# A transformer block on one core: self-attention's output projection in seven half-size products over pairs of units

## The chip, the core and the metric

The kernel runs on one NeuronCore of a Trainium2 chip. A core has five engines that work side by side, each in the order of its own instruction queue: TensorE (PE in the profile; PEld is its loading of weights) multiplies matrices out of on-chip memory (SBUF) into eight accumulation banks (PSUM); VectorE (DVE), ScalarE (ACT) and GpSimd (POOL) work on rows of 128 partitions; SyncE (SP) issues the transfers, which 16 DMA engines carry out. Engines wait for each other through semaphores. The metric is the time of one execution on the device in microseconds (us), the median of three runs. All data are 32-bit floats; a 32-bit product shows as two matmul records in the trace.

## What is computed

The reference, cut to what matters:

```python
h = layernorm(x, ln1);  x = attention(h, h, sa_wq, sa_wk, sa_wv, sa_wo, sa_bo) + x
h = layernorm(x, ln2);  x = attention(h, cond, ca_wq, ca_wk, ca_wv, ca_wo, ca_bo) + x
h = layernorm(x, ln3);  p = h @ ff_w1 + ff_b1
a, gate = p[..., :1024], p[..., 1024:]
out = (a * gelu(gate)) @ ff_w2 + ff_b2 + x

def attention(xq, xkv, wq, wk, wv, wo, bo):     # 16 heads of 64
    q, k, v = xq @ wq, xkv @ wk, xkv @ wv
    return softmax(q k^T / 8, per head) v @ wo + bo
```

x is 2 x 1024 x 256 (two batches of 1024 tokens), the context 2 x 154 x 192, the attention width 1024. The output projection `@ wo` takes 1024 values a token to 256, and its result is added to x.

## The kernel before

**Units and steps.** The self-attention goes by 16 *units*: a batch b and a pair of heads pr (8 pairs a batch). A unit is 8 *steps*, so the stage has 128 (`SA`), numbered p; n is the step within a unit, ui the unit. In step p the main loop first does `self_first`: TensorE multiplies the scores of two groups of 64 query rows, for two heads and 1024 keys, into two PSUM tiles of 128 x 1024 (`scores`, L502); VectorE takes the maxima (L511); ScalarE takes the exponentials with their sums (L517); SyncE sends maxima and sums between partitions in four small transfers, the *exchange* (L527); one step later GpSimd works out differences and denominators (L535 to L546), two steps later VectorE takes reciprocals (L614) and GpSimd multiplies the weights (`weighted`, L622), and VectorE turns them (L649) into the tile that the value products read (L556). At the end of a step TensorE gets one more piece of work: the value products of half a half-unit (64 products, steps 0, 3, 4 and 7 of a unit), or, in steps 1, 2, 5 and 6, what `run_work` takes from the lists `work` (the next unit's queries, keys and values), `side` (normalizations of the other batch or the next stage) and `outs` (output projections). Order on each engine is the program's order.

**The output projection.** The 8 pairs of a batch make four groups `og` of two pairs (`HP` = 2, `NQ` = 4). Outputs of a group are kept transposed in a tile `oT` of 2 x 1024 columns (two buffers in rotation), its weights in a tile `wo` of 2 x 256 columns (two buffers, `load_out`). When a group is done, `self_beside` appends `out_piece`s, two in each of the next two units: a piece takes two token tiles of 128, four products of 256 columns (L476), and one addition to x on VectorE (L483), which the main loop does one step later from `adds`. They run in step 6 of units 2 to 14 and step 2 of unit 15; the last group of batch 1 runs as four pieces early in the cross-attention.

**The cross-attention** goes by the same 16 units in 48 steps c (three a unit): scores on context keys `kT` (L876), softmax without an exchange, turned weights, value products (L941), queries of the next unit, output projections. The context keys of pairs 0 to 5 are made during the first self-attention units, those of pairs 6 and 7 in its last step but one (p = SA - 2). `kT` holds all of them, 8 x 320 columns, in SBUF for both stages. At the end the feed-forward takes its two products in seven half-size products for eight (L1046, L1167), in the manner of Strassen and Winograd; `kT` then serves it as a buffer.

**Biases** are added to x on GpSimd (L323) from the list `later`, one at steps 2, 4 and 6 from unit 4 on. **Transfers** all go through SyncE's queue in the program's order, with eight semaphores in rotation. `load_ahead` places the weights of the unit after next at steps 2, 3 and 7, and the output weights at step 6 of every second unit. Normalized inputs of a stage are in tiles `hT`, one for each batch (two buffers): batch 0's self-attention tile is followed in its buffer by batch 0's cross-attention tile.

Of the kernel before, what the change touches and what calls it, by code (L numbers as in the profile page):

```python
# [13 lines left out]
P = 128  # L14
# [4 lines left out]
def tile_transformer_block(ctx: ExitStack, tc: tile.TileContext, a: dict, out: bass.AP):  # L19
# [165 lines left out]
    kT = const.tile([P, NPAIR, B * TP], F32, tag="kT", name="kT")  # L185

# [34 lines left out]
    def norm_pieces(kind, b, first=False):  # L221
# [11 lines left out]
        def stats(t):  # L233
            if t == 0:
                st["hT"] = hT[kind, b] = p2.tile(
                    [P, nh, NC * S // nh], F32, tag="hT", name=f"hT_{ln}_{b}")
# [39 lines left out]
        def turn(t):  # L276
# [10 lines left out]
            def store():  # L287
                k = NC * 2 * P // nh
                for c in range(nh):
                    own = st["hT"][:, c, t // 2 * k:(t // 2 + 1) * k]  # L290
# [38 lines left out]
    def norm_beside(kind, b):  # L329
# [12 lines left out]
        for k in range(NT // n + 3):  # L342
            tiles = tile_order(kind)[k * n:(k + 1) * n]
            needs = [(after, b, half, t) for half in range(NQ) for t in tiles if after]
# [16 lines left out]
    def two_banks(name):  # L361
        return [mm_tile(f"{name}_{r}") for r in range(2)]
# [79 lines left out]
    def self_queries(b, pr, m=KB, t0=0):  # L442
        pq = two_banks(f"pq_sa{b}_{pr}")
# [227 lines left out]

    def self_values(h, part):

        b, pr = units[h // 2]
        if part == 0:
            halves[h, "po"] = [sum_tile(f"po_{h}_{a2}") for a2 in range(2)]
            if pr % HP == 0 and h % 2 == 0:
                oT["sa", b, pr // HP] = pt_.tile([P, HP, S], F32, tag="oT", name=f"o_sa{b}_{pr}")
# [43 lines left out]
    def self_beside(ui):  # L722
# [16 lines left out]
        if ui == NPAIR + 1:  # L739
            norm_beside("ca", 0)  # L740

    def load_ahead(p):
# [19 lines left out]
        if p == SA - SH - 6:  # L762
            load_keys(6, 2)

# [94 lines left out]
    def cross_pieces(b, pr):  # L859

        return [
            costing(2, lambda: cross_queries(b, pr, KB)),
# [3 lines left out]
    def cross_first(c):  # L866
# [4 lines left out]
        q, k = qk["ca", b, pr], kT[:, pr, b * TP:b * TP + T]  # L871
        sc = ps_s.tile([P, 2, HB], F32, tag="s", name=f"sc_{c}")
# [329 lines left out]
    with tc.manual_schedule():  # L1202
# [61 lines left out]
        for p in range(SA):  # L1264
# [16 lines left out]
            load_ahead(p)  # L1281
            if p < 2 * SH - 1 or p % SH in (1, 2):

                run_work(2 if p < SA - SH else 1, n > SH or p < SH, sum_tile)
# [4 lines left out]
                elif p == SH + 2:  # L1289
                    run(lambda: together(*(  # L1290
                        lambda pr=pr: context_keys(pr, sum_tile) for pr in (3, 4))))
                    flush(stores)
                elif p == SA - 2:
                    run(lambda: context_values(*units[0]))
                    for pr in (6, 7):
# [175 lines left out]
```

## Time and profile before

| | us |
|---|---|
| median of 3 runs | 1072.77 (1072.15 to 1073.38) |
| the profiled execution | 1073.1 |
| its span, first to last instruction | 1071.3 |
| TensorE busy | 1059.9 (99%) |
| VectorE busy | 879.9 (82%) |
| GpSimd busy | 766.8 (72%) |
| ScalarE busy | 653.3 (61%) |
| self-attention's output projection, TensorE busy | 59.8, 256 records of 386 ns |
| feed-forward's second product in half-size products, TensorE busy | 58.5 over five groups, 448 records of 275 ns |

Busy time is the union of an engine's records, each with its modelled end; consecutive records overlap, so durations of single matmuls add up to more than the time they take, and the distance between starts is the better measure of pace. "A <-B" behind an idle time names what ended it. In a list of groups the columns are line, engine, operation, output <- inputs with shapes, count, busy time and mean, and idle time before them; in a timeline, start, duration, engine and line; in the chain of waits, start, duration and what the end of the program was waiting for. A row of the stretches gives the busy time of PE, PEld, DVE, ACT and POOL with counts, then the granted clock, the DMA share and GB/s.

### The profile page before, as it was taken

Reading aid. Unit: us, or ns where it says so; the run is one execution under the profiler, and the core shown is the slowest. Engines: PE = TensorE matmul, PEld = TensorE weight load, DVE = VectorE, ACT = ScalarE, POOL = GpSimd, SP = SyncE. Lnnn points to the kernel's source line nnn. Section 1 sums busy time; section 2 is a strip of 40 time slices with the busy share of each in tenths; the row PEclk is TensorE's granted clock in tenths of the full one; section 3 lists DMA queues with packets and bytes.
Section 4 is the critical chain, followed back from the end, with each engine's and each line's share of the span. In section 5 each row is a group of like instructions: output and inputs, shape, how many; then the busy total and the mean of one; then the engine's idle time right before and its main releaser. Section 6 shows DMA issues by size and latency. Waiting matters only on the chain.

```text
span 1071.3 us, 46097 instructions
## 1 busy us (share of the span) xinstructions
PE 1059.9 (99%) x19108; PEld 707.8 (66%) x19108; DVE 879.9 (82%) x1293; ACT 653.3 (61%) x2089; POOL 766.8 (72%) x1604
## 2 busy tenths in 40 slices
PE   8999999999999999999999999999999999999998
PEld 6545557566566565665665656566777767889998
DVE  5789999998989989989999898978776777765654
ACT  5666767667766666666667766666556655243221
POOL 2677777778777777777776776758766678598783
PEclk9999999999999999999999999999999999999999
DMA  3232122111111111211211211125523221000000
GB/s 95 64 92 64 46 48 46 34 44 24 43 43 35 43 44 25 58 30 35 48 31 34 48 29 38 24 68 132 131 60 83 68 58 41 1 6 16 21 10 31
DMA packets 99235, 50.57 MB, mean 47 GB/s; under 512 B 30218, under 2 KB 97810, under 8 KB 99026
## 3 DMA queue, kind: packets, MB, share of 16 engines
q1 hardware_dynamic: 97698, 46.96, 17.9%
q8 instruction: 151, 2.47, 1.0%
q10 hardware_dynamic: 1328, 0.66, 0.2%
q14 instruction: 58, 0.48, 0.2%
HBM read 35.25 MB, written 3.41 MB: 36 GB/s over the span
## 4 chain that ended last, share of the span: by engine, by line
PE 89%; DVE 4%; ACT 2%; POOL 2%; DMA 1%; issue 1%; SPq 1%; DVEq 0%; POOLq 0%; ACTq 0%
PE s L502 20%; PE po L556 19%; PE py_sa L476 5%; PE py_ca L476 5%; PE pv_sa L402 5%; PE pq_sa L371 5%; PE pk_sa L371 5%; PE pf L1167 4%; PE pq_ca L371 4%; PE poc L941 4%; PE pb L1046 4%; PE sc L876 3%; PE pa L1046 2%; PE pc L1046 2%; DMA st<-st 1%; PE ph_ln L283 1%
## 5 line engine op out<-in xcount | busy, mean ns | idle before, releaser
L622 POOL TENSOR_SCALAR p<-p,rd,ee 128x512 f32<-128x512 f32 x508 | 386.4, 771 | 96.9 <-DVE rd L614 93.7
L517 ACT ACTIVATE p<-s,st 128x512 f32<-128x512 f32 x512 | 345.7, 686 | 178.0 <-DVE st L511 174.7
L511 DVE TENSOR_REDUCE st<-s 128x2 f32<-128x1024 f32 x256 | 308.4, 1206 | 52.5 <-issue 20.4
L649 DVE STREAM_TRANSPOSE pT<-p 128x1024 f32<-128x1024 f32 x256 | 302.2, 1218 | 1.5 <-POOL p L622 1.5
L502 PE MATMUL s<-k_sa,q_sa 64*32 64x512 f32 x4096 | 255.2, 591 | 2.6 <-ACT p L517 1.9
L556 PE MATMUL po<-pT,v_sa 64*32 64x256 f32 x8192 | 238.6, 376 | 0.8 <-ACT p L894 0.8
L556 PEld LDWEIGHTS po<-pT,v_sa 64*32 64x32 f32 x8192 | 175.2, 106 | 72.9 <-issue 26.8
L502 PEld LDWEIGHTS s<-k_sa,q_sa 64*32 64x32 f32 x4096 | 81.4, 106 | 103.1 <-issue 54.0
L894 ACT ACTIVATE p<-sc,neg 128x154 f32<-128x154 f32 x256 | 97.1, 405 | 72.2 <-DVE rden L902 65.8
L905 POOL TENSOR_SCALAR p<-p,rden 128x154 f32<-128x154 f32 x256 | 97.2, 404 | 52.5 <-DVE rden L902 51.6
L517 ACT ACTIVATION_READ_ACCUMULATOR p<-s,st 128x1 f32 x512 | 103.4, 202 | 0.0
L535 POOL TENSOR_TENSOR dd<-st 128x8 f32<-128x8 f32 x128 | 26.0, 203 | 68.9 <-DMA st<-st 65.0
L402 PEld LDWEIGHTS pv_sa<-sa_wv,hT_ln 64*128 64x128 f32 x1024 | 58.5, 188 | 14.2 <-issue 10.1
L881 DVE TENSOR_REDUCE neg<-sc 128x6 f32<-128x924 f32 (+1 forms) x48 | 48.1, 1002 | 20.2 <-PE sc L876 20.0
L402 PE MATMUL pv_sa<-sa_wv,hT_ln 64*128 64x128 f32 x1024 | 61.7, 275 | 0.0
L476 PE MATMUL py_ca<-ca_wo,o_ca 128*128 128x256 f32 x256 | 61.1, 385 | 0.0
L476 PE MATMUL py_sa<-sa_wo,o_sa 128*128 128x256 f32 x256 | 59.8, 386 | 0.0
L476 PEld LDWEIGHTS py_sa<-sa_wo,o_sa 128*128 128x128 f32 x256 | 47.2, 190 | 18.0 <-ACT v_sa L411 5.9
L371 PE MATMUL pq_ca<-hT_ln,ca_wq 64*128 64x512 f32 (+1 forms) x352 | 57.7, 589 | 0.0
L371 PE MATMUL pq_sa<-hT_ln,sa_wq 64*32 64x512 f32 (+1 forms) x976 | 57.2, 586 | 0.0
L371 PE MATMUL pk_sa<-hT_ln,sa_wk 64*32 64x512 f32 x960 | 56.6, 590 | 0.0
L894 ACT ACTIVATION_READ_ACCUMULATOR p<-sc,neg 128x1 f32 x256 | 56.5, 221 | 0.0
(132 smaller groups left out, 1451.0 us busy)
## 6 DMA issues: line engine op xcount, KB each, us to landing
v_sa<-v_sa SPq DMA_DIRECT2D x32, 256.0 KB, 3.8
st<-st SPq DMA_DIRECT2D x510, 1.0 KB, 1.8
v_ca<-vd SPq DMA_DIRECT2D x32, 160.0 KB, 3.4
sa_wq<-in_L_xattn_sa_wq_dram SPq DMA_DIRECT2D x32, 128.0 KB, 3.6
sa_wk<-in_L_xattn_sa_wk_dram SPq DMA_DIRECT2D x32, 128.0 KB, 3.6
sa_wv<-in_L_xattn_sa_wv_dram SPq DMA_DIRECT2D x32, 128.0 KB, 3.3
ca_wq<-in_L_xattn_ca_wq_dram SPq DMA_DIRECT2D x32, 128.0 KB, 3.4
wf<-in_L_xattn_ff_w_dram SPq DMA_DIRECT2D x12, 256.0 KB, 5.9
```

Source lines behind the costliest of these rows:

```text
L371: nc.tensor.matmul(pq[r][f:f + m, at:at + n], lhsT=wt[own, c, f:f + m], rhs=h[own, c, t0:t0 + n], start=(c == 0), stop=(c == NH - 1), tile ...
L402: nc.tensor.matmul(pv[r][:, i * P:(i + 1) * P], lhsT=h[own, c, i * P:(i + 1) * P], rhs=wt[own, c, :], start=(c == 0), stop=(c == NH - 1), ...
L476: nc.tensor.matmul(py[:, e * D:(e + 1) * D], lhsT=o[:, i, (t + e) * P:(t + e + 1) * P], rhs=wo[kind, b, g][:, i, :], start=(i == 0), stop= ...
L502: nc.tensor.matmul(sc[a4 * KB:(a4 + 1) * KB, j, :], lhsT=q[r, c:c + KB], rhs=k[r, h * HB:(h + 1) * HB], start=True, stop=True, tile_positi ...
L511: nc.vector.tensor_reduce(st[:, 0, 0, i, :], sc, AX.X, ALU.max, negate=True)
L517: nc.scalar.activation(pr[:, j, :], sc[:, j, :], AF.Exp, bias=st[:, 0, 0, i, j:j + 1], accum_out=st[:, 0, 1, i, j:j + 1],)
L556: nc.tensor.matmul(po[a2][d:d + KB, :QH // 2], lhsT=v[r, t, e, d:d + KB], rhs=pT[r, d // DH * NK + n, :], start=(t == 0 and e == 0), stop= ...
L622: nc.gpsimd.tensor_scalar(pr[:, j, :], pr[:, j, :], v["rd"][:, c:c + 1], v["ee"][:, 0, c:c + 1], op0=ALU.mult, op1=ALU.mult,)
L649: nc.vector.transpose(halves[h][:, :, c:c + KB], slot[p]["members"][i].rearrange("p j (n k) -> p (j n) k", k=KB))
L894: nc.scalar.activation(pr_[:, j, i, :T], sc[:, j, i * T:(i + 1) * T], AF.Exp, bias=neg[:, j, i:i + 1], accum_out=den[:, j, i:i + 1],)
L905: nc.gpsimd.tensor_scalar(pr_[:, j, i, :T], pr_[:, j, i, :T], rden[:, j, i:i + 1], 1.0, op0=ALU.mult, op1=ALU.mult,)
L1046: nc.tensor.matmul(into[:, :BT], lhsT=lhs, rhs=wh[pair][i], start=first, stop=True, skip_group_check=True)
```

## The change

A batch's four groups make two halves of two groups. Batch 0's two halves and batch 1's first (groups 0 and 1) are now projected in seven half-size products instead of eight; batch 1's second half stays in whole pieces.

A *block* n takes two token tiles (t0 and t0 + 2) and the two groups of a half as a 2 x 2 matrix of blocks A, and the two groups' weights, each split into its left and right 128 columns, as B. `weight_blocks` makes five sums of B on GpSimd once for a half, `token_blocks` five sums of A on GpSimd for each block, `out_block` multiplies seven products of 128 columns (two instructions each) into two PSUM tiles, and returns three functions that add the results to x on VectorE: one addition of 512 columns and four of 256, in three steps one after another.

Block n belongs to unit n + 4, so blocks 0 to 11 run in units 4 to 15; their products are emitted in step 6 (the last one in step 2 of unit 15), their GpSimd sums one to two in a step from step 0 on. Both weight tiles of a half are loaded in step 7 of units 3, 7 and 11. Units 2 and 3 have no output projection. Batch 1's groups 2 and 3 are eight whole pieces from the first step of the cross-attention on.

Since outputs of two groups must be kept for four units more, four homes hold them: groups 0 and 1 in the two `oT` buffers, group 2 in `kT`'s first 2048 columns, and group 3 in the batch's own `hT` buffer (`homes`), which the last unit's projections no longer need. So the context keys are all made by step 22, stored in device memory (`kd`) at step 24, and loaded back whole at cross step 6; the first four units' keys come back into small tiles near the end of the self-attention. The rest of `kT` and a part of `ends` hold weight sums, the tile of context-key weights holds token sums. Queries of the self-attention and the first cross unit use the value banks (`sum_tile`), so that the two `mm` banks can hold a block's results. The second normalization takes the token tiles in another order, and starts in unit 10 in place of 9.

The diff, cut to its core:

```diff
+    kd = dram.tile([P, NPAIR, B * TP], F32, name="kd")
+    homes = [p2.tile([P, NC * S], F32, tag="hT", name=f"home{b}") for b in range(B)]
@@ tile_order
+        if kind == "ca":
+            return [t for r in range(TF) for i in range(r, NT // 2, TF) for t in (i, NT // 2 + i)]
+    def parts_of(kind, b):
+        if kind == "sa":
+            return ("s0", "s1") if b < B - 1 else ("s0", NQ - 2, NQ - 1)
+        return range(NQ)
@@ self_pieces
-            return self_queries(b, pr)
+            return self_queries(b, pr, bank=sum_tile)
+    def hold_outputs(b, og):
+        if og == NQ - 2:
+            flat = kT.rearrange("p a b -> p (a b)")[:, :HP * S]
+        elif og == NQ - 1:
+            flat = homes[b]
+        else:
+            oT["sa", b, og] = pt_.tile([P, HP, S], F32, tag="oT", name=f"o_sa{b}_{og}")
+            return
+        oT["sa", b, og] = flat.rearrange("p (i s) -> p i s", i=HP)
+    NBLK = NT // 2
+    def weight_blocks(n):
...
+        tt = nc.gpsimd.tensor_tensor
+        return [
+            lambda: tt(t1, b11, b22, ALU.add),
+            lambda: tt(t3, b12, b22, ALU.subtract),
+            lambda: tt(b12, b11, b12, ALU.add),
+            lambda: tt(t4, b21, b11, ALU.subtract),
+            lambda: tt(b21, b21, b22, ALU.add),
+        ]
+    def token_blocks(n):
...
+        return [
+            lambda: tt(s1, a11, a22, ALU.add),
+            lambda: tt(s2, a21, a22, ALU.add),
+            lambda: tt(s5, a11, a12, ALU.add),
+            lambda: tt(a21, a21, a11, ALU.subtract),
+            lambda: tt(a12, a12, a22, ALU.subtract),
+        ]
+    def out_block(n):
...
+        for own, at, m in ((px, 1, 3), (px, 2, 4), (px, 3, 6), (px, 0, 7), (py, 0, 1), (py, 1, 5), (py, 2, 2)):
+            for c in range(HP):
+                nc.tensor.matmul(
+                    own[:, at, :], lhsT=sums_t[n][m][:, c, :], rhs=sums_w[m][:, c, :],
+                    start=(c == 0), stop=(c == HP - 1), skip_group_check=True)
...
+        def first():
+            take(square, px.rearrange("p (j d) k -> p j d k", d=2))
+        def second():
+            take(diagonal, px[:, 2:0:-1, :])
+            take(diagonal, py[:, 0:1, :].broadcast_to([P, 2, P]))
+        def third():
+            take(other, py[:, 1:3, :])
+            take(diagonal, py[:, 1:3, :], ALU.subtract)
@@ self_beside
-        if ui >= HP:
-            ob, og = divmod((ui - HP) // HP, NQ)
-            t0 = (ui % HP) * 2
-            out_pieces("sa", ob, og, out_order("sa")[t0:t0 + 2])
@@ load_ahead
-        if n == 2 * SH - 2 and ui % HP == 1 and p < SA - 2:
-            k = ui // HP
-            load_out("sa", *divmod(k, NQ))
+        half = ui // NBLK
+        if n == 2 * SH - 1 and ui % NBLK == NBLK - 1 and ui < NU - 1:
+            for og in range(2 * half % NQ, 2 * half % NQ + 2):
+                load_out("sa", 2 * half // NQ, og)
+        if p == SA - SH - 1:
+            for og in (NQ - 2, NQ - 1):
+                load_out("sa", B - 1, og)
-        if p == SA - SH - 6:
+        if p == 2 * SH + 1:
             load_keys(6, 2)
+        if p == 6 * SH:
+            nc.sync.dma_start(out=kd, in_=kT)
+        if p == SA - 2 * SH:
+            crossed["first"] = one.tile([P, 3, TP], F32, tag="xn", name="k_first")
+            nc.sync.dma_start(out=crossed["first"], in_=kd[:, :3, :TP])
+        if p == SA - SH - 1:
+            nc.sync.dma_start(out=ends[:, HP * P:HP * P + TP], in_=kd[:, 3, :TP])
@@ the main loop, self-attention
+            block, at = ui - NBLK, n
+            if block == NU - NBLK - 1 and n != 2:
+                block = None
+            elif block == NU - NBLK - 2 and n == 2 * SH - 1:
+                block += 1
+            if block is not None and block >= 0:
+                if n == 0 and block % NBLK == 0:
+                    summing.extend(weight_blocks(block))
+                if n == (2 * SH - 1 if block == NU - NBLK - 1 else 0):
+                    summing.extend(token_blocks(block))
+            steps = 2 if ui >= NU - 1 or n == 2 * SH - 1 else -(-len(summing) // max(6 - n, 1))
+            for _ in range(min(steps, len(summing))):
+                summing.pop(0)()
             if p < 2 * SH - 1 or p % SH in (1, 2):
-                run_work(2 if p < SA - SH else 1, n > SH or p < SH, sum_tile)
+                if block is not None and block >= 0 and n == (2 if ui == NU - 1 else 2 * SH - 2):
+                    adds.extend(out_block(block))
+                turns = n > SH or p < SH or n == 2 and NU - NBLK <= ui < NU - 1
+                run_work(2 if p < SA - SH else 1, turns, sum_tile)
+                elif p == 5 * SH + 2:
+                    run(lambda: together(*(
+                        lambda pr=pr: context_keys(pr, sum_tile) for pr in (6, 7))))
                 elif p == SA - 2:
                     run(lambda: context_values(*units[0]))
-                    for pr in (6, 7):
-                        run(lambda: context_keys(pr, sum_tile))
@@ the main loop, cross-attention
+                for og in (NQ - 2, NQ - 1):
+                    out_pieces("sa", B - 1, og, out_order("sa"))
             if c == SH:
-                out_pieces("sa", B - 1, NQ - 1, out_order("sa"))
             if c == 0:
                 run(lambda: self_values(2 * NU - 2, 1))
+                run_work(2, 0)
-                if ui > 1:
+                if ui:
                     run_work(0, 0, n_sum=1)
-            if c == 0:
-                load_out("sa", B - 1, NQ - 1)
+            if c == 2 * len(CG):
+                nc.sync.dma_start(out=kT, in_=kd)
```

More of the change, by code (lines that the diff above doesn't have):

```diff
@@ L289, in store @@
                 for c in range(nh):
-                    own = st["hT"][:, c, t // 2 * k:(t // 2 + 1) * k]
+                    at = t // 2 if kind == "ff" else order[t] % (NT // 2)
+                    own = st["hT"][:, c, at * k:(at + 1) * k]
                     turned = ph[c * n // nh][:, c % (nh // n) * k:][:, :k]
@@ L343, in norm_beside @@
             tiles = tile_order(kind)[k * n:(k + 1) * n]
-            needs = [(after, b, half, t) for half in range(NQ) for t in tiles if after]
+            needs = [(after, b, half, t) for half in parts_of(after, b) for t in tiles if after]
             def step(fns):
@@ L677, in self_values @@
             if pr % HP == 0 and h % 2 == 0:
-                oT["sa", b, pr // HP] = pt_.tile([P, HP, S], F32, tag="oT", name=f"o_sa{b}_{pr}")
+                hold_outputs(b, pr // HP)
         po = halves[h, "po"]
```

53 lines of the change are left out of this document (45 added, 8 removed).

## The prediction

> **What bounds the kernel now.** I read first the share of the span by engine and the chain of work that ended last, on the page: the span is 1071.3 us, the same execution took 1073.1 us (1.8 us lie around the span), and the median of the runs shown is 1072.77, so a sum made on this execution is lowered by 0.3 us at the end. About 0.2%, 2.1 us, is what a measurement of this kernel can tell from no change.
>
> ```profile
> PE 1059.9 (99%) x19108; PEld 707.8 (66%) x19108; DVE 879.9 (82%) x1293; ACT 653.3 (61%) x2089; POOL 766.8 (72%) x1604
> PE 89%; DVE 4%; ACT 2%; POOL 2%; DMA 1%; issue 1%; SPq 1%; DVEq 0%; POOLq 0%; ACTq 0%
> ```
>
> TensorE is the chain almost everywhere, at full clock. Next come the timelines of one self-attention step (unit 8, its first step), engine by engine: a step is two score groups, then either 64 value products or a projection or an output projection.
>
> ```profile
> 350.19 1.95 PE L502 MATMUL s<-k_sa,q_sa 64*32 64x512 f32 x32
> 352.07 3.72 PE L476 MATMUL py_sa<-sa_wo,o_sa 128*128 128x256 f32 x16
> 355.72 1.95 PE L502 MATMUL s<-k_sa,q_sa 64*32 64x512 f32 x32
> 360.91 1.92 PE L502 MATMUL s<-k_sa,q_sa 64*32 64x512 f32 x32
> 366.08 1.92 PE L502 MATMUL s<-k_sa,q_sa 64*32 64x512 f32 x32
> ...
> 362.17 1.21 DVE L511 TENSOR_REDUCE st<-s 128x2 f32<-128x1024 f32 x1
> 363.30 0.15 DVE L614 RECIPROCAL rd<-den 128x4 f32<-128x4 f32 x1
> 366.77 0.65 DVE L483 TENSOR_TENSOR x<-py_sa,x 128x512 f32<-128x512 f32 x1
> 367.34 1.21 DVE L511 TENSOR_REDUCE st<-s 128x2 f32<-128x1024 f32 x1
> ```
>
> A plain step is 366.08 - 360.91 = 5.17 us of TensorE; the one with the output projection is 355.72 - 350.19 = 5.53. VectorE needs, without the addition, 366.77 - 362.17 = 4.60 us, and 5.17 with it (367.34 - 362.17). So TensorE bounds the stage, VectorE is 0.57 us behind it, and a step that TensorE has less for can shrink by that and no further than 4.60.
>
> **The change part by part.**
>
> *The products.* Each of 12 blocks replaces 8 products of 256 columns (two records each) by 14 of 128 columns. That is 16 records against 28, in the same slot of a unit. The second kind is seen in the feed-forward, in the chain's own view:
>
> ```profile
> 1043.30 0.89 PE pf L1167 x8
> 1055.83 11.22 PE pf L1167 x98
> 307.21 0.59 PE ph_ln L283 x4
> ...
> L476 PEld LDWEIGHTS py_sa<-sa_wo,o_sa 128*128 128x128 f32 x256 | 47.2, 190 | 18.0 <-ACT v_sa L411 5.9
> ```
>
> The long run gives 11.22/98 = 0.1145 us a record, 3.21 for 28; a run that follows the narrow score tiles pays an entry (four transposes of the same shape took 0.59 where 0.45 is due), so I take 3.29 against 5.53 - 1.88 = 3.65 now, -0.36 a block, **-4.3 us**. Ends: 3.12 (the eight-record run) gives -6.4, and 3.35 gives -3.6. [...]
>
> *Units 2 and 3.* They held two output projections each and now hold none (blocks run in units 4 to 15). Their step 6 falls from 5.53 to VectorE's 4.60 at best: -0.93 each, and 0 at worst; I take **-1.5 us** together, since VectorE waits a little in most steps. Context keys 6 and 7 go into unit 2's emptied slot and cost nothing there.
>
> *Four more output projections in the cross-attention.* The last half of batch 1 stays in whole products: eight pieces now run after the self-attention, where four did.
>
> ```profile
> 693.52 2.32 PE L786 MATMUL pk<-ctxT,ca_wk 96*128 96x320 f32 x8
> 711.56 0.80 PE L556 MATMUL po<-pT,v_sa 64*32 64x256 f32 x17 [0.85 <-ACT p L894]
> ...
> 716.23 3.61 PE po L556 x128
> ...
> 720.83 3.65 PE py_sa L476 x16
> ...
> 725.21 1.92 PE py_sa L476 x8
> ...
> 722.00:760.00 38.00, 37.91 (x447) 26.35 (x446) 31.37 (x74) 23.92 (x115) 29.09 (x76) 1.00 0.49 124
> ```
>
> TensorE works 37.91 of 38 us there, so nothing hides them. Two pieces at the first cross step cost 3.65, less the 0.85 us gap that they fill, less at most 0.5 for the context keys (2.32 us) that leave the last self step but one, which VectorE then holds at 4.60. Two more come one at a time, at cross steps 5 and 8: 1.85 each. Together **+5.9 us** (ends 4.5, if the chain through ScalarE hides a piece, and 7.4, all four).
>
> So TensorE alone comes out level: -4.3 - 1.5 + 5.9 = +0.1.
>
> *The sums on GpSimd.* Each block adds five additions of 128x256, and the first block of a half five more on its weights: 75 in all.
>
> ```profile
> L323 POOL TENSOR_TENSOR x<-x,sa_bo 128x256 f32<-128x256 f32 x16 | 11.7, 733 | 0.0
> ...
> 400.54 1.52 POOL L622 TENSOR_SCALAR p<-p,rd,ee 128x512 f32<-128x512 f32 x2 [0.81 <-DMA st<-st]
> 404.32 0.20 POOL L546 TENSOR_TENSOR den<-zz 128x4 f32<-128x4 f32 x1
> 405.72 1.52 POOL L622 TENSOR_SCALAR p<-p,rd,ee 128x512 f32<-128x512 f32 x2 [1.20 <-DVE rd L614]
> ```
>
> GpSimd's own step is 404.52 - 400.54 = 3.98 us, so 1.2 of 5.17 are free and one addition of 0.73 fits: nine units place one in each of five steps, hidden, **+0.4 us** where a bias addition falls into the same step (ends 0 and 3). In units 4, 8 and 12 two additions stand in each of four steps, 1.45 us, 0.26 too much each time, and the first waits for both weight matrices, which SyncE now issues one step before, behind the exchange and the value weights.
>
> ```profile
> 364.21 1.36 SPq L134 DMA_DIRECT2D sa_wv<-in_L_xattn_sa_wv_dram  x2
> sa_wo<-in_L_xattn_sa_wo_dram SPq DMA_DIRECT2D x8, 256.0 KB, 3.6
> wf<-in_L_xattn_ff_w_dram SPq DMA_DIRECT2D x12, 256.0 KB, 5.9
> 367.70 0.20 POOL L546 TENSOR_TENSOR den<-zz 128x4 f32<-128x4 f32 x1
> 368.73 1.52 POOL L622 TENSOR_SCALAR p<-p,rd,ee 128x512 f32<-128x512 f32 x2 [0.84 <-DVE rd L614]
> ```
>
> In unit 8's first step SyncE is free at 365.57; two issues of 0.6 and 3.6 to landing put the second matrix at 369.85, where GpSimd, at the end of its step, wants it at 367.90. Queued behind the waiting addition are the weightings of the next step, due at 368.73, then the differences and denominators; VectorE's reciprocal and transposes wait for those, ScalarE for VectorE, TensorE for ScalarE. Two additions end at 371.30: GpSimd is 2.6 late. A matrix that lands 1.2 sooner gives 1.4; I take 1.9. The three further double steps add 0.26 each, in units 4 and 8 also 0.72 for a bias addition and 0.26 for the next: 3.7, 3.7 and 2.7 late. What of that TensorE feels:
>
> ```profile
> 404.33 1.20 DVE L511 TENSOR_REDUCE st<-s 128x2 f32<-128x1024 f32 x1
> 256.78 0.18 DVE L614 RECIPROCAL rd<-den 128x4 f32<-128x4 f32 x1 [0.79 <-POOL den L546]
> 258.93 1.77 PE s L502 x31
> 260.70 3.77 PE pv_sa L402 x64
> ```
>
> A reciprocal follows the first maximum by 1.13 (362.17 to 363.30 above), so here at 405.46, 0.9 after its denominators; in unit 5 it waited another 0.79, and the chain of waits still stayed on TensorE. So about 1.7 us of lateness are free, and TensorE loses 2.0 + 2.0 + 1.0 = **+4.9 us** (ends: 0.6, if the matrices are there when wanted, since only the 0.26s and the biases then add up; 11, at the 5.9 to landing of the second row).
>
> *Keys through device memory.* One store of 1.25 MB at step 24, two small loads, and the whole load at cross step 6. The nearest row is the crowd of 1.25 MB in the first unit:
>
> ```profile
> 53.76 1.07 SPq L797 DMA_DIRECT2D ca_wv_ends<-in_L_xattn_ca_wv_dram  x2
> 56.44 4.32 SPq L527 DMA_DIRECT2D st<-st  x4
> 60.24 3.46 DMA st<-st
> ```
>
> There the four issues of an exchange took 4.3 us and the last one's landing 3.46, and the chain went through it. Here the store stands alone, with no other load in its step and in a unit without additions: **+0.2**, ends 0 and 3. [...] The reload has six cross steps until unit 4 reads it: **+0.1**, ends 0 and 2.
>
> *No cost.* Two rows for what is hidden:
>
> ```profile
> 709.04 0.53 ACT o_sa L688 x2
> L1176 DVE TENSOR_TENSOR x<-pf,x 128x256 f32<-128x256 f32 x8 | 3.4, 421 | 2.8 <-PE pf L1167 2.8
> ```
>
> Queries now use the value banks, which two copies (0.53 us) empty while TensorE does the 1.9 us of scores; uncovered, that is 0.5 in a unit. A block's results come in five additions, one of 512 and four of 256 columns, over three steps: 5.17, then twice at most 4.60 + 0.84 = 5.44 against TensorE's 5.17, which the next steps give back; uncovered, 0.5 a block. The new order of the cross-attention's normalization has the same operations, due by unit 15.
>
> Sum: 0.1 + 0.4 + 4.9 + 0.3 = +5.7 on 1073.1, less 0.3: **1078.5 us**.
>
> **The rivals.**
>
> *GpSimd's lateness is absorbed.* Landing at 368.7 and a little more slack leave only TensorE's sum and the small terms: 1072.8 to 1074. For it: GpSimd often waits for the exchange anyway (0.81 in the row above). Against: two additions a step exceed the room in any case.
>
> *Faster: the moved pieces are hidden.* From the last self step on, the chain leaves TensorE for the softmax that drains (the copies at 709.04 above lie on it). If all four pieces fell into that, the 5.9 would go: -4.3 - 1.5, and with GpSimd at its low ends (+0.6, +0.3) some 4.9 below the execution, about 1068; it decides from two hidden pieces on. Against it: 37.91 of 38 us, and one gap of 0.85.
>
> *GpSimd becomes the bound of the three double units.* Both matrices land 5.9 us after issue: +11 in place of 4.9, and the exchange queued behind them is late too: about 1085.
>
> *The seven products save nothing.* If weight loads of 0.19 us (the PEld row above) could not hide behind 128 columns, a block would take 28 x 0.19 = 5.3 us: +20 and 1098. The run of 98 records at 0.1145 speaks against it.
>
> **How the numbers follow.** The forecast has 0.55, the absorbed case 0.2, the faster one 0.13, the slow one 0.1, the last 0.02. The range from 1070.5 to 1084.5 leaves out about 0.2. Faster by over 0.2%: 0.14; within: 0.18; slower: 0.68.
>
> **What would show it.** The step from a block's scores to the next should be 5.15 to 5.2 us (now 5.53). GpSimd's first weight addition in units 4, 8 and 12 should show an idle time before it, put down to the load of the output weights, and TensorE's next four steps should be longer by 2 us in sum. Units 2 and 3 should be 0.7 to 0.9 shorter, and from the last self step to the third cross unit some 6 us more should pass. Wrong would be: no idle time before that addition, or a cross stage that isn't longer.

## The result and the profile after

The changed kernel takes 1100.66 us (median of 4 runs, 1099.22 to 1101.64), the kernel before 1073.08 beside it: ratio 1.0257, interval 1.0240 to 1.0275. The direction was forecast; the size was not: +27.6 in place of +5.4 (1078.5 less 1073.08), outside the range. The profiled execution took 1099.22 (span 1097.3), 26.1 more than that of before, where the working had +5.7.

Share of the span by engine, and the granted clock in 40 slices, from the page of the changed kernel:

```profile
PE 1068.7 (97%) x19252; PEld 711.8 (65%) x19252; DVE 892.1 (81%) x1329; ACT 652.7 (59%) x2089; POOL 815.5 (74%) x1679
...
PEclk9999999999999999999999999899999999999999
```

TensorE now idles 28.6 us of its span (11.4 before), and one slice has an 8 where before had 9 everywhere. The list of waits, TensorE's rows (engine, line, what ended the wait; total, times, longest):

```profile
PE s L512 <- ACT p L527: 6.3, 12, 2.3
PE pq_ca L381 <- DVE x L756: 4.7, 1, 4.7
PE ph_ln L284 <- POOL xn_ln L271: 3.4, 4, 1.8
PE pk_sa L381 <- DVE x L756: 2.1, 2, 1.1
...
PE p_rows L195 <- ACT q_sa L396: 1.6, 1, 1.6
PE po L566 <- ACT kT L897: 1.6, 1, 1.6
```

Most rows are one wait or a few, at single places. Where the time went, by stretches: units 0 and 1; 2 and 3; 4 to 14; unit 15 to the first cross scores; cross-attention to its last scores. Columns: stretch, length, then busy times; the clock stands third from the end. The kernel before, then the changed one:

```profile
17.43:104.33 86.90, 84.96 (x1666) 46.07 (x1674) 68.80 (x76) 57.88 (x171) 52.22 (x110) 1.00 0.27 64
104.33:189.86 85.53, 85.53 (x1964) 52.08 (x1956) 79.42 (x94) 60.07 (x177) 63.56 (x135) 1.00 0.20 48
189.86:659.36 469.50, 469.50 (x10772) 285.24 (x10764) 430.93 (x489) 321.24 (x944) 353.13 (x732) 1.00 0.17 38
659.36:701.10 41.74, 41.74 (x933) 22.84 (x917) 39.63 (x45) 27.80 (x86) 31.38 (x66) 1.00 0.10 25
701.10:899.96 198.86, 197.51 (x2543) 140.69 (x2536) 148.78 (x313) 124.30 (x576) 139.02 (x367) 1.00 0.34 86
```

```profile
17.48:105.58 88.10, 85.39 (x1665) 49.42 (x1673) 68.89 (x76) 58.01 (x171) 52.07 (x110) 1.00 0.27 66
105.58:192.71 87.13, 82.97 (x1941) 52.00 (x1932) 78.73 (x92) 60.35 (x178) 63.18 (x133) 0.98 0.22 58
192.71:668.86 476.15, 471.26 (x10905) 281.49 (x10897) 438.67 (x517) 321.00 (x942) 399.13 (x801) 1.00 0.16 38
668.86:719.06 50.20, 44.17 (x936) 21.53 (x920) 41.21 (x51) 27.22 (x84) 34.58 (x72) 0.93 0.14 35
719.06:926.08 207.02, 204.70 (x2575) 147.14 (x2568) 152.16 (x317) 124.16 (x577) 139.15 (x367) 1.00 0.33 88
```

The differences are +1.2, +1.6, +6.65, +8.5 and +8.2; what follows is unchanged (-0.1). The products themselves came as forecast. Unit 9's step 6 in the changed kernel, TensorE's timeline:

```profile
441.26 1.95 PE L512 MATMUL s<-k_sa,q_sa 64*32 64x512 f32 x32
443.14 0.71 PE L747 MATMUL px<-kT 128*128 128x128 f32 x4
...
445.48 1.06 PE L747 MATMUL py<-sa_wo,sums_t 128*128 128x128 f32 x8
446.46 1.09 PE L512 MATMUL s<-k_sa,q_sa 64*32 64x512 f32 x16
```

446.46 - 441.26 = 5.20 us, 0.33 under the 5.53 of before; so the products alone give units 4 to 14 11 x 0.33 = 3.6, and 10.3 were lost to something else.

The largest single loss is unit 15's step 5, 13.05 us (5.15 before). TensorE and VectorE there, then TensorE's clock in stretches of 3.41 us, first around unit 3's step 6, then around that wait:

```profile
695.15 2.17 PE L512 MATMUL s<-k_sa,q_sa 64*32 64x512 f32 x32
696.90 0.38 DVE L756 TENSOR_TENSOR x<-x,px 128x256 f32<-128x256 f32 x1
697.31 0.42 DVE L756 TENSOR_TENSOR x<-x,py 128x256 f32<-128x256 f32 x1
...
699.98 2.36 DVE L659 STREAM_TRANSPOSE pT<-p 128x1024 f32<-128x1024 f32 x2
702.26 0.71 DVE L756 TENSOR_TENSOR x<-x,py 128x256 f32<-128x256 f32 x2
703.03 6.00 PE L381 MATMUL pq_ca<-home,ca_wq 64*32 64x512 f32 x55 [4.66 <-DVE x L756]
```

```profile
183.02:186.44 3.42, 1.08 (x24) 0.18 (x16) 3.42 (x5) 3.38 (x11) 3.08 (x8) 1.00 0.32 58
186.44:189.85 3.41, 3.31 (x48) 1.12 (x48) 3.33 (x7) 2.06 (x6) 2.22 (x6) 0.50 0.46 100
...
698.43:701.85 3.42, 0.00 (x0) 0.00 (x0) 3.42 (x5) 2.88 (x9) 2.31 (x5) 1.00 0.21 58
701.85:705.26 3.41, 2.23 (x24) 0.67 (x32) 1.13 (x3) 0.00 (x0) 1.52 (x4) 0.50 0.11 25
705.26:708.68 3.42, 3.42 (x40) 0.88 (x32) 0.00 (x0) 0.00 (x0) 0.00 (x0) 0.50 0.00 0
708.68:712.09 3.41, 3.41 (x50) 1.20 (x34) 1.60 (x3) 1.43 (x3) 0.19 (x1) 1.00 0.00 0
```

The second cross query projection (`pq_ca`) needs both `mm` banks. Block 11's third addition, which reads the second one, stands on VectorE behind the maxima and transposes of the same step, so the bank is free at 703; the scores of the next step stand behind the projection on TensorE. TensorE idles for 4.66 us; from 701.85 us on the clock is at 0.50 for two stretches, 6.83 us, and the projection's 55 records take 5.8 us of starts, where the same 55 take 3.03 in experiment e2 at 1.00. Theory: the held bank costs 4.7 us, the half clock that follows about 3 more.

### The profile page after: what moved, and what is told of

Read it like the earlier page. It is cut to its first block, busy times and chain, and to the rows that moved or that the text cites. A ratio compares the mean times of both kernels' runs of the same rounds, so it can differ in the third digit from the quotient of the medians.

```text
span 1097.3 us, 46504 instructions
## 1 busy us (share of the span) xinstructions
PE 1068.7 (97%) x19252; PEld 711.8 (65%) x19252; DVE 892.1 (81%) x1329; ACT 652.7 (59%) x2089; POOL 815.5 (74%) x1679
## 5 line engine op out<-in xcount | busy, mean ns | idle before, releaser
L512 PE MATMUL s<-k_sa,q_sa 64*32 64x512 f32 x4096 | 261.7, 594 | 7.4 <-ACT p L527 6.3
L566 PE MATMUL po<-pT,v_sa 64*32 64x256 f32 x8192 | 241.3, 377 | 1.6 <-ACT kT L897 1.6
L566 PEld LDWEIGHTS po<-pT,v_sa 64*32 64x32 f32 x8192 | 178.3, 106 | 73.0 <-issue 26.2
L412 PEld LDWEIGHTS pv_sa<-sa_wv,home 64*128 64x128 f32 x1024 | 58.5, 188 | 14.2 <-issue 10.1
L381 PE MATMUL pq_ca<-home,ca_wq 64*128 64x512 f32 (+1 forms) x352 | 61.6, 658 | 4.7 <-DVE x L756 4.7
L412 PE MATMUL pv_sa<-sa_wv,home 64*128 64x128 f32 x1024 | 61.7, 275 | 0.0
L381 PE MATMUL pk_sa<-home,sa_wk 64*32 64x512 f32 x960 | 57.9, 590 | 2.1 <-DVE x L756 2.1
L381 PE MATMUL pq_sa<-home,sa_wq 64*32 64x512 f32 (+1 forms) x976 | 57.0, 586 | 0.0
L1032 DVE STREAM_TRANSPOSE pT_ca<-p 128x480 f32<-128x480 f32 (+1 forms) x96 | 52.8, 586 | 0.1
L486 PEld LDWEIGHTS py_ca<-ca_wo,o_ca 128*128 128x128 f32 x256 | 46.9, 190 | 7.7 <-issue 1.8
```

What stands on the lines that cost most here:

```text
L381: nc.tensor.matmul(pq[r][f:f + m, at:at + n], lhsT=wt[own, c, f:f + m], rhs=h[own, c, t0:t0 + n], start=(c == 0), stop=(c == NH - 1), tile ...
L412: nc.tensor.matmul(pv[r][:, i * P:(i + 1) * P], lhsT=h[own, c, i * P:(i + 1) * P], rhs=wt[own, c, :], start=(c == 0), stop=(c == NH - 1), ...
L486: nc.tensor.matmul(py[:, e * D:(e + 1) * D], lhsT=o[:, i, (t + e) * P:(t + e + 1) * P], rhs=wo[kind, b, g][:, i, :], start=(i == 0), stop= ...
L512: nc.tensor.matmul(sc[a4 * KB:(a4 + 1) * KB, j, :], lhsT=q[r, c:c + KB], rhs=k[r, h * HB:(h + 1) * HB], start=True, stop=True, tile_positi ...
L566: nc.tensor.matmul(po[a2][d:d + KB, :QH // 2], lhsT=v[r, t, e, d:d + KB], rhs=pT[r, d // DH * NK + n, :], start=(t == 0 and e == 0), stop= ...
```

## The experiments

Each ratio is to the kernel before, timed beside the experiment on the same chip; experiments of different chips compare by it. Stretches and steps are those of one profiled execution each.

**Unit 15: the bank and the clock.** Experiment e1 ends block 11's additions one step sooner:

```diff
             if adds:
                 adds.pop(0)()
+            if p == SA - SH and adds:
+                adds.pop(0)()
```

> The last block's second and third additions both follow in the step after the first, one step sooner. Theory 'held bank': in step 5 of unit 15 TensorE waits 4.7 us for the bank that the third addition still reads, and the half clock after it costs 3 more; so that step falls from 13.05 to between 5.2 and 5.8 us, its clock is 1.00, and the whole goes from 1100.7 to about 1093. Rival 'all are late there' (the exchange or the weights of the query projection set that step): the step stays above 11 us and the whole within 1 us of 1100.7.

Measured: 1093.16 us, ratio 1.0188 (1.0172 to 1.0203). Step 5 of unit 15 takes 6.00, a little over the 5.2 to 5.8 expected, at a clock of 1.00:

```profile
698.41 1.08 DVE L756 TENSOR_TENSOR x<-x,py 128x256 f32<-128x256 f32 x3
698.43 4.35 PE L381 MATMUL pq_ca<-home,ca_wq 64*32 64x512 f32 x57
```

The projection follows the additions without idling. The step is 7.0 us shorter and the whole 7.5: that much of the loss is this bank, shown.

Experiment e2 leaves the waits and fills them with work that nothing reads:

```diff
+                if p == 6 * SH + 6:      # unit 3, step 6: 8 records
+                    idle = mm_tile("idle3")
...
+                if p == SA - SH + 1:     # unit 15, step 5: a projection twice
+                    project_both(two_banks("idle15", sum_tile), wsl["ca", units[1][1], "q"], ...)
```

> Adds products that nothing reads: 8 records (1.85 us) in the emptied step 6 of unit 3, and a whole second query projection (64 records, 3.4 us) before the one that waits in step 5 of unit 15. Theory 'idle halves the clock': with TensorE kept busy the clock stays at 1.00; unit 3's last two steps go from 11.38 to about 9.7 us, unit 15's step 5 from 13.05 to about 10.1, the whole from 1100.7 to about 1096, with more work. Rival 'the clock falls for another reason' (load, time of the run): the steps stay or grow, by up to 3.4 us in unit 15, and the whole is 1100 to 1104.

Measured: 1098.44, ratio 1.0231 (1.0216 to 1.0246). Unit 15's step 5 is 10.32 us and unit 3's last two steps 10.32 (4.65 + 5.67), both at a clock of 1.00. Unit 15 in e2's timeline:

```profile
699.56 3.64 PE L381 MATMUL idle<-home,ca_wq 64*32 64x512 f32 x64
702.99 1.02 PE L381 MATMUL pq_ca<-home,ca_wq 64*32 64x512 f32 x2
704.71 0.71 DVE L756 TENSOR_TENSOR x<-x,py 128x256 f32<-128x256 f32 x2
705.48 3.23 PE L381 MATMUL pq_ca<-home,ca_wq 64*32 64x512 f32 x55 [1.47 <-DVE x L756]
```

The same 55 records take 3.2 us behind a busy TensorE, where they took 6.0: more work, 2.7 us less. Here the half clock came with the idling and not with the amount of work. The whole gained 2.2 and not 4.6: units 4 to 14 of this execution were longer by 3.4, for which I have no cause.

**Units 2 and 3: an emptied slot.** Experiment e5 takes the kernel before and only empties the slots:

```diff
-        if ui >= HP:
+        if ui == HP:
+            added.update(("sa", 0, 0, t) for t in range(NT))
+        if ui >= 2 * HP:
             ob, og = divmod((ui - HP) // HP, NQ)
```

> The kernel before, with the output projections of the first group (step 6 of units 2 and 3, four products of each of 16 records) left out, so 0.4% of the output's work is missing and nothing is added. The prediction's step 'an emptied slot shortens its unit by 0.93 at best': units 2 and 3 together 1.5 to 1.9 shorter (85.54 to about 83.8), the whole 1073.1 to about 1071.4. Theory 'the next scores wait for their bank, and what stands behind them waits too': step 6 falls to 4.2 to 4.6 us, but step 7 grows by 0.5 to 2 us, the two units change by -0.9 to +1.3 in sum, the whole is 1072.2 to 1074.4; the wait before step 7's second scores is put down to ScalarE.

Measured: ratio 1.0012 (1.0000 to 1.0024), with work left out. In the profiled execution the two units took 87.82 us against 85.53, more than even the theory's 1.3. (That execution also lost 2.8 us after the self-attention: its span is 5.0 longer than that of before, and its step 127 ends 2.14 later. Its mean clock, 0.995 over 1076.3 us, leaves some 3 us or more at half clock outside the self-attention's steps. So its whole is no measure of the slots.) TensorE in unit 2's steps 6 and 7 of e5, and the clock there:

```profile
140.50 1.09 PE L502 MATMUL s<-k_sa,q_sa 64*32 64x512 f32 x16 [2.33 <-ACT p L517]
...
143.50 4.58 PE L556 MATMUL po<-pT,v_sa 64*32 64x256 f32 x128
```

```profile
138.51:141.92 3.41, 1.18 (x24) 0.27 (x32) 3.41 (x5) 2.88 (x9) 3.23 (x7) 1.00 0.42 93
141.92:145.34 3.42, 3.42 (x56) 1.61 (x64) 3.36 (x7) 2.13 (x5) 2.34 (x6) 0.50 0.49 107
```

TensorE comes early to the next scores, waits for a bank that ScalarE's exponentials still read, and the value products queued behind the scores can't use the time. Step 6 shrinks from 5.53 to 4.28 us, and step 7 grows from 5.19 to 7.36. TensorE was busy throughout the half-clock stretch, 3.42 us; half of that, 1.7, is by estimate its part of the 2.2. Unit 3 has another such stretch, 186.29 to 189.71, with 3.35 us busy at 0.50. An estimate without the two, 87.82 - 2 x 1.7 = 84.4, is 1.1 under before: by it the slots gain nearly what was forecast, and the half clock behind their idling takes more, 3.4. The term "-1.5" came out with the wrong sign.

**GpSimd's additions.** Experiment e4 leaves all 75 out:

```diff
     def weight_blocks(n):
-        return [lambda: tt(t1, b11, b22, ALU.add), ...]      # five
+        return []
     def token_blocks(n):
-        return [lambda: tt(s1, a11, a22, ALU.add), ...]      # five
+        return []
```

> Leaves out all 75 additions on GpSimd; the products take the blocks themselves, so the output projection of 12 blocks is not the reference's. Theory 'GpSimd makes VectorE late': units 4 to 14, 476.2 us together, fall to about 466 and the whole from 1100.7 to about 1090; no wait of the key projections for the block's additions is left in units 8 and 12. Rival 'banks and the moved normalization': they fall by less than 4 us.

Experiment e10 leaves out the 15 on weights alone (`weight_blocks` returns five empty functions).

> Leaves out the 15 additions on the weights (products take the blocks themselves), so the output projection of 12 blocks is not the reference's; the token additions keep their places, one to a step. Theory 'weights: wait and double steps': units 4 to 14, 476.2 us, fall to within 1 us of the 469.5 that all additions left out gave. Rival 'token additions cost as much': they stay above 472.5.

Measured: 1092.28 and 1093.16. Units 4 to 14 of e10:

```profile
193.80:663.31 469.51, 468.17 (x10905) 282.76 (x10896) 438.16 (x517) 321.18 (x942) 390.64 (x787) 1.00 0.17 38
```

e4 has 469.45, e10 469.51: the 60 token additions cost nothing, the 15 on weights 476.15 - 469.51 = 6.6 us (4.9 was forecast). These are single executions: e1, e2 and e3, whose edits lie in other units, took 475.87, 479.60 and 474.76 there, so by these the size lies between 5 and 10. e4 also shows that 3.6 are lost to neither kind of addition: 469.5 equals before, although the products save 3.6.

Part of these 3.6 can be placed. In e4, e10 and e15 (the last experiment, without additions too) step 3 of unit 8 is 0.8 to 1.05 us longer than before. In e10, SyncE and GpSimd ahead of it:

```profile
368.55 1.99 SPq L162 DMA_DIRECT2D sa_wo<-in_L_xattn_sa_wo_dram  x2
375.79 0.20 POOL L545 TENSOR_TENSOR dd<-st 128x8 f32<-128x8 f32 x1 [2.11 <-DMA st<-st]
```

The exchange stands in SyncE's queue behind the loads of both weight tiles, and GpSimd waits 2.11 us for it, where before it waited 0.15. No run moved these loads alone, so this is read from the trace and not shown.

What of the weights costs? In the changed kernel GpSimd's first weight addition of units 4, 8 and 12 waits 2.47, 1.93 and 2.12 us (1.95 was worked out). From the timeline:

```profile
201.78 0.73 POOL L713 TENSOR_TENSOR kT<-sa_wo,sa_wo 128x256 f32<-128x256 f32 x1 [2.47 <-DMA sa_wo<-in_L_xattn_sa_wo_dram]
374.57 0.74 POOL L713 TENSOR_TENSOR kT<-sa_wo,sa_wo 128x256 f32<-128x256 f32 x1 [1.93 <-DMA sa_wo<-in_L_xattn_sa_wo_dram]
544.94 0.74 POOL L713 TENSOR_TENSOR kT<-sa_wo,sa_wo 128x256 f32<-128x256 f32 x1 [2.12 <-DMA sa_wo<-in_L_xattn_sa_wo_dram]
```

Experiment e9 removes that wait and keeps the additions:

```diff
+                late = int(block % NBLK == 0)
-                if n == 0 and block % NBLK == 0:
+                if n == late and block % NBLK == 0:
                     summing.extend(weight_blocks(block))
-                if n == (2 * SH - 1 if block == NU - NBLK - 1 else 0):
+                if n == (2 * SH - 1 if block == NU - NBLK - 1 else late):
```

> In units 4, 8 and 12 the ten additions start one step later (steps 1 to 5, two in each), when both weight matrices have landed; nothing else. Theory 'the wait for the load': GpSimd's idle of 1.9 to 2.5 us before the first weight addition goes, and units 4, 8 and 12 (44.41, 44.47, 46.71, together 135.6) fall to about 132; the whole by 3 to 4. Rival 'two additions in a step exceed the room, wherever they stand': the three units stay within 1 us of 135.6 or grow, since five steps now hold two.

Measured: 1099.54, ratio 1.0243 (1.0228 to 1.0258). The three units of e9:

```profile
193.03:237.35 44.32, 43.29 (x1001) 24.40 (x985) 37.88 (x45) 29.41 (x85) 40.23 (x79) 1.00 0.19 46
365.42:410.79 45.37, 43.57 (x996) 24.78 (x988) 39.93 (x46) 28.06 (x84) 38.83 (x76) 1.00 0.18 45
536.65:582.73 46.08, 43.92 (x1004) 26.64 (x996) 41.74 (x53) 31.88 (x95) 39.48 (x79) 1.00 0.18 44
```

135.8 against 135.6: no wait is left before the first addition, and nothing is gained. The rival holds: ten additions in five steps exceed GpSimd's room. In unit 4 steps 2 to 4 are regular again, but now the products of step 6 wait for the last of them (7.09 us in unit 8, where 5.20 is usual).

Experiment e6 frees the banks one step sooner in every block, and loads the first weights two steps earlier:

```diff
-        return [first, second, third]
+        return [first, lambda: (second(), third())]
...
-        if n == 2 * SH - 1 and ui % NBLK == NBLK - 1 and ui < NU - 1:
+        if n == 2 * SH - (3 if half == 0 else 1) and ui % NBLK == NBLK - 1 and ui < NU - 1:
```

> Two edits in different units: a block's additions take two steps in place of three, so the banks are free one step sooner; and the first half's weights are loaded in step 5 of unit 3 in place of 7. Theory 'banks': step 2 of unit 8 falls from 6.45 to about 5.2, step 2 of unit 12 from 8.04 to about 6.2, step 5 of unit 15 from 13.05 to about 6.0. Theory 'the late load': GpSimd's idle before unit 4's first weight addition (2.47) goes and steps 2 to 4 of unit 4, 16.93, fall by 0.8 to 1.4. Whole: about 1089. Rival 'GpSimd's number of additions sets units 4, 8 and 12, not bank or load': those steps stay within 0.4, only unit 15 falls, and the whole is about 1093.

Measured: 1094.26, ratio 1.0167 (1.0145 to 1.0188). Unit 15's step 5 is 5.33. Units 8 and 12 are not shorter (44.97, 46.84). TensorE's waits in unit 8, changed kernel and then e6:

```profile
PE pk_sa L381 <- DVE x L756: 1.1, 1, 1.1
```

```profile
PE s L512 <- ACT p L527: 1.2, 4, 0.3
```

The wait for the bank goes, and the scores wait as long for exponentials. By these lists VectorE is late behind GpSimd, and the bank was only where it showed. In unit 4 steps 2 to 4 fall from 16.93 to 15.84 and step 1 takes back 0.46. In the five versions with the early load (e6, e7, e8, e11, e12) unit 4 takes 42.9 to 43.9 us, against 44.4 to 45.3 in the four that have all additions in their old places and the late load (the changed kernel, e1, e2, e3). So an earlier load helps, by 0.5 to 2 us, where a later start (e9) doesn't: by this reading, what counts is the time from the landing to the products. For units 8 and 12 it would need two more weight buffers; it wasn't tried.

**Three other places** that were costed at nothing, undone in experiment e3:

```diff
-            return self_queries(b, pr, bank=sum_tile)
+            return self_queries(b, pr, bank=mm_tile if (b, pr) == units[1] else sum_tile)
...
-                        lambda pr=pr: context_keys(pr, sum_tile) for pr in (6, 7))))
+                        lambda pr=pr: context_keys(pr, mm_tile) for pr in (6, 7))))
...
-        if kind == "ca":
+        if kind == "ca" and b < B - 1:
             return [t for r in range(TF) ...]
```

> Three edits undone, each read in its own steps: unit 1's queries use the mm banks again (in unit 0), context keys 6 and 7 are made in mm banks, batch 1's second normalization takes its tiles in the old order. Theory 'each costs where it stands': step 3 of unit 0 from 7.14 to about 5.5, step 7 of unit 2 from 7.25 to about 5.7, cross step 11 from 6.76 to about 4.8; the whole from 1100.7 to about 1096. Rival 'TensorE's idle there is given back by the step after, or is due to the moved pieces': each of the three stays within 0.5 us in its sum over three steps, and the whole within 1 us.

Measured: 1094.01, ratio 1.0200 (1.0183 to 1.0217). Unit 0's step 3 is 5.48 again (a *turn* is a transposition on TensorE; in the changed kernel that of the row tile waited 1.59 there for a value bank that the queries held), unit 2's step 7 is 5.69, cross step 11 is 5.15. Unit 3 grew by 1.1 (its steps 0 and 1 by 1.3), so most of unit 2's gain is given back. Cross step 11, changed kernel and e3:

```profile
774.83 0.66 PE L284 MATMUL ph_ln<-ident,xn_ln 128*128 128x128 f32 x4 [1.82 <-POOL xn_ln L271]
```

```profile
769.02 0.63 PE L284 MATMUL ph_ln<-ident,xn_ln 128*128 128x128 f32 x4 [0.25 <-ACT q_ca L396]
```

In the new order batch 1's second pair of token tiles needs the last moved pieces, so its normalization starts late and its turn waits for GpSimd. The three places give 3.6 of the 5.8 us between the two profiled executions. Another 1.1 are unit 15's half clock, which was shorter in this execution: step 5 took 11.94 us at a mean clock of 0.86, that is some 3.3 us at half in place of 6.83.

Experiment e13 takes the kernel before and gives batch 0's normalization the change's timing:

```diff
-        if ui == NPAIR + 1:
+        if ui == NPAIR + 2:
...
-                run_work(..., n > SH or p < SH, sum_tile)
+                run_work(..., n > SH or p < SH or n == 2 and NU - 4 <= ui < NU - 1, sum_tile)
```

> The kernel before, with only the timing of batch 0's second normalization taken from the change: it starts in unit 10 in place of 9 and may turn its tiles in step 2 of units 12 to 14 too. Theory 'a turn in step 2 costs more than one in step 5' (1.1 against 0.6 us, and it makes step 5 later): units 11 to 14, 171.8 us, grow by 1.0 to 2.5, and the whole to 1074.5 to 1075.5. Rival 'a turn costs 0.6 wherever it stands': units 11 to 14 and the whole stay within 0.5 us.

Measured: ratio 1.0022 (1.0013 to 1.0032); units 11 to 14 take 173.37 in place of 171.76. So 1.6 of the 3.6 are the moved turns: shown. Of the other 2.0, about 1 is the step of unit 8 above; the rest stays open.

**Together.** Experiment e7 joins e6, e3 and unit 3's filling records:

> All mends together: additions in two steps, the early first load, 8 filling records in step 6 of unit 3, unit 1's queries and context keys 6 and 7 in mm banks, batch 1's second normalization in the old order. Theory 'the costs are separate places': 1100.7 - 7.5 (unit 15) - 4 (units 4, 8, 12) - 5 (places) - 1 (unit 3) = about 1083, no half clock before the end. Rival 'mending one place moves the wait to the next': above 1087.

Experiment e8 leaves out the store and the reload besides (its two lines, and other data in the small loads):

> e7 without the store of the keys at step 24 and without their reload; the cross-attention reads other data as keys, with as many small loads. The prediction's price of 0.3 for both: the whole within 0.5 us of e7. Rival 'the store delays the exchange of unit 3's first two steps': 1.0 to 2.5 us faster than e7, in steps 0 and 1 of unit 3.

Measured on one chip, where the kernel before took 1075.64: 1089.76 (1.0131, 1.0114 to 1.0147) and 1089.83 (1.0129, 1.0111 to 1.0147). The device-memory trip costs nothing that these intervals, some 2 us to each side, can tell from zero. e7's rival holds: units 8 and 12 didn't get shorter.

Experiment e11 is e7 with e1's edit of the additions in place of e6's, and e9's edit in units 8 and 12:

> The mends that held, together: the last block's additions in two steps (those of the other blocks in three), first weights loaded in step 5 of unit 3, sums of units 8 and 12 one step later, 8 filling records in unit 3, unit 1's queries and keys 6 and 7 in mm banks, batch 1's second normalization in the old order. If the waits are separate: before x 1.010 (about 1084); if a mended wait moves on to the next step: as the first mended version, before x 1.013 (1087 or more).

Experiment e12 also starts the turns in unit 13:

```diff
-                turns = n > SH or p < SH or n == 2 and NU - NBLK <= ui < NU - 1
+                turns = n > SH or p < SH or n == 2 and NU - NBLK < ui < NU - 1
```

> As the run ahead of it, and the extra normalization turns in step 2 start in unit 13 in place of 12. Theory 'a turn beside late sums costs twice in unit 12': unit 12 (46.7 in the changed kernel) falls by a further 1.5 to 2.5 us, the units behind it grow by at most 0.6, the whole is 1 to 2 us under that run. Rival 'a turn costs 0.6 wherever it stands': the two runs agree within 0.5 us.

Measured: 1086.21 (1.0118, 1.0102 to 1.0135) and 1085.00 (1.0112, 1.0097 to 1.0127). e11 lies between its two expectations and decides for neither. From e11 to e12 unit 12 falls by 2.5 and unit 13 grows by 2.3: the turn's cost moves with it, and the 1.2 between the two runs is inside their intervals. Last, a second look at e12, and e12 without GpSimd's additions:

> A second look at e12 beside the next run, for the sums: about 1085.

> e12 with all 75 additions on GpSimd left out as well (products take the blocks themselves, so the projection of 12 blocks is not the reference's). Theory 'the design's floor lies above the kernel before': cross-attention +6.5, products -4, turns +1 to +2.5, so about 1077 (1076 to 1079). Rival 'without GpSimd's sums the seven products pay': 1073 or less.

Measured beside 1074.64: 1085.61 and 1082.24 (1.0073, 1.0058 to 1.0088). By the ratio e15 is 2 to 4 us above its expectation: its units 4 to 14 take 470.93 us, so the unassigned 2 us and a little more stand here again. Still, this most mended version lies above the kernel before even with free sums: what lies behind unit 14, with the four moved pieces in it, is 7.1 us longer (419.0 against 411.9 to the span's end), and the products save 3.6.

## Why the prediction was wrong

| place | forecast | measured | shown by |
|---|---|---|---|
| products in units 4 to 14 | -4.0 | -3.6 | steps of 5.20 |
| GpSimd's sums there | +5.3 | +6.6 | e4, e10 |
| the rest there (store, turns) | +0.2 | +3.6 | e13 for 1.6; 2.0 not shown |
| units 0 and 1 | 0 | +1.2 | e3 |
| units 2 and 3 | -1.5 | +1.6 | e5, e2 |
| unit 15 to the first cross scores | -0.9 | +8.5 | e1, e2 |
| cross-attention | +6.5 | +8.2 | e3 for 1.6 |

Forecasts sum to 5.6 (the forecast's 12th block and the leaving context keys stand in unit 15, the reload in the cross-attention), measured terms to 26.1.

*Right.* The products: 5.20 was forecast as 5.15 to 5.2, and a block's 28 records take 446.46 - 443.14 = 3.32 us (3.29 was taken). The blocks' loads of 128 columns are recorded at 190 to 192 ns (medians), and the records of this block start 0.119 us apart on average (3.32/28), so here loads and products overlapped. The four pieces: from the first cross scores to the tenth step the stage took 43.68 us against 37.38, +6.3 for a forecast of 6.4. The keys' trip: nothing measurable, for 0.3. GpSimd's idle before the weight additions was there, at 1.9 to 2.5 us, and the sum of its lateness was near (5.3 for 6.6). That nearness is luck in part: half of the lateness was put down to the wait for the load, and without that wait the units were to lose 0.6; e9 took it away and gained nothing. Unit 12 was put at half of unit 8 and was not less.

*The step that failed: "No cost".* Three of its items cost some 12 of the missing 20 us. "A block's results come in five additions ... over three steps ... uncovered, 0.5 a block" priced VectorE's time, and not how long the two banks stay taken. In most units nothing wants them in those steps; in unit 15, where the block stands in step 2 and a projection that kept the `mm` banks in step 5, their next user waited 4.7 us, with everything queued behind it, and the half clock behind it added about 3 (step 5 grew by 7.9, and e1 took 7.0 of it back). "Queries now use the value banks ... uncovered, that is 0.5 in a unit" overlooked another user of these banks in unit 0 (1.2). "The new order of the cross-attention's normalization has the same operations" counted operations, not their places: batch 1's cost 1.6 in the cross-attention (e3), and the later start and places of batch 0's turns 1.6 (e13).

*The second: units 2 and 3*, "at best: -0.93 each, and 0 at worst". The worst was wrong. The order of TensorE's queue turned the emptied slot into idling, 2.33 us in unit 2 of e5, and the clock behind it was at 0.50: two stretches in e5, 3.4 us by estimate, more than the slots gain (+2.3 in sum), and one, 1.7 us, in the changed kernel. Where the slot was filled and the clock stayed at 1.00 (e2), unit 3 took 42.64 us against 43.00 before. The context keys, which were to "cost nothing there", also held a bank for which the value products waited 1.6 us (`po` behind `kT` in the list of waits); e3 got 0.8 of that back over the two units.

None of the rivals had this; the dearest that was near in size (products that save nothing, 1098) is refuted by the 5.20.

## What to carry to other kernels

When results move to other accumulation banks or stay in them longer, list for every bank who asks for it next in each irregular place (first unit, last unit, stage change); the copying engine's time is not the price, the asking engine's queue is. An emptied slot on the bounding engine is a full gain only if what follows can move up; otherwise part of it is idling, and here the half clock behind the idling took an estimated 3.4 us (e5) where the two slots gained 1.1. Work placed beside an engine's room must fit step by step: one GpSimd addition in each step was free sixty times, two in a step cost 6.6 us for fifteen more, and starting them a step later gained nothing.

## What the runs showed of the hardware

TensorE's clock behind its idling, as three of the executions recorded it, in stretches of 3.41 to 3.44 us:

| execution | stretch | clock in it | TensorE idle in it, us | clock in the next 3.4 us |
|---|---|---|---|---|
| changed kernel, unit 3 | 183.02 to 186.44 | 1.00 | 2.34 | 0.50 |
| changed kernel, unit 15 | 698.43 to 701.85 | 1.00 | 3.42 | 0.50 |
| changed kernel, unit 15 | 701.85 to 705.26 | 0.50 | 1.18 | 0.50 |
| changed kernel, unit 15 | 705.26 to 708.68 | 0.50 | 0 | 1.00 |
| e5, unit 2 | 138.51 to 141.92 | 1.00 | 2.23 | 0.50 |
| e5, unit 3 | 182.88 to 186.29 | 1.00 | 2.32 | 0.50 |
| e4, unit 3 | 181.20 to 184.64 | 1.00 | 1.55 | 1.00 |
| e4, unit 3 | 184.64 to 188.05 | 1.00 | 1.36 | 1.00 |

The last two are one wait of 2.67 us and a short one behind it, and the clock stays:

```profile
181.20:184.64 3.44, 1.89 (x33) 0.43 (x32) 3.31 (x7) 3.25 (x10) 3.19 (x8) 1.00 0.03 3
184.64:188.05 3.41, 2.05 (x40) 0.60 (x48) 3.38 (x5) 2.50 (x9) 3.32 (x7) 1.00 0.73 153
188.05:191.46 3.41, 3.41 (x141) 2.64 (x132) 3.36 (x6) 2.99 (x7) 1.86 (x4) 1.00 0.06 9
```

So a wait of some 2.3 to 2.7 us was followed by half clock in the changed kernel and in e5, and not in e4; at half clock, 3.4 us of work are by estimate 1.7 us lost. Each row is one execution, and no run varied the length or the place of an idle alone: what decides between the two cases is not shown.
